# Gathers on GpSimd: rows ahead of values, early messages for 14 row blocks, and a pause behind two of three gathers

## The chip, the cores and the metric

The kernel runs on one core of a Trainium2 chip. The metric is the device time in microseconds of one execution. Work is spread by hand over the engines: PE (TensorE, matrix products), DVE (VectorE), ACT (ScalarE), POOL (GpSimd) and the DMA queues. Each engine works through its own queue of instructions in order and waits on semaphores of the others.

## The reference

Two graph layers over 2708 nodes with 128 features. `adj` is a 2708 x 2708 matrix that is almost empty: a few neighbours a row, each row's non-zero entries equal (one over their number).

```python
# layer 0, for x (2708, 128)
XW = mobius_matvec(W, x)                       # x @ W, rescaled row by row
gamma = 2 / max(1 - sum(XW * XW), eps)
two_mean = (adj @ (gamma * XW)) / clamp(adj @ (gamma - 1))
AXW = mobius_scalar_mul(adj.sum(-1), mobius_scalar_mul(0.5, two_mean))
x = layernorm(x + expmap0(relu(logmap0(AXW))))

# layer 1
s, d = x @ msg_w[:, :D].T, x @ msg_w[:, D:].T
messages = gelu(s[i] + d[j] + msg_b)           # for every pair i, j
aggregated[i] = sum_j messages[i, j] * adj[i, j]
new = concat(x, aggregated) @ upd_w.T + upd_b
x = layernorm(x + layernorm(gelu(new) + x) * ln_w + ln_b)
```

The messages are needed for the non-zero entries of `adj` alone. The kernel finds these entries on the device while it does layer 0, and computes layer 1 edge by edge.

## The kernel before, in words

Rows are cut into 22 blocks of 128.

**Layer 0.** `layer0(b)` loads the transposed block of `adj` (tile `aT`, two buffers, 1.4 MB, on the SyncE queue), multiplies it with `y` in 22 products of 128 x 130 (L369) and writes the block's nominator and denominator into `nom[:, b]` (L374, one VectorE operation a block, which is a handy clock of the progress). ScalarE takes the sign of `aT` (L364).

**Finding the edges.** `keys` turns the signs into numbers that hold column positions (L396 and the following lines) and takes the largest eight of each group (L404). `extract` makes from these a list of edges for the block, in *edge tiles* of 128 edges each: `J` (the neighbour's number), `rid` (the row within the block) and `same` (the weight of the row). Block 0 has 20 such tiles, block 1 has 8, later ones fewer; there are 99. `F` (12 buffers, L501) is the place of each edge in `adj`. A first part of each block's tiles holds only edges to the first ten blocks of columns ("early" tiles, 51 in all); the rest are "late".

**Gathers.** `gather` starts an indirect DMA on GpSimd's queue (L197): each of the 128 partitions fetches from an address of its own. There are two kinds, 99 of each:
- values, `V<-adj,F`: one number for each edge, read back from `adj` and compared at the end with `same`, to make sure that the found edge has the weight that was assumed;
- rows, `dd<-table,J`: 128 numbers for each edge, the neighbour's `d`, out of the DRAM tensor `table`.

Values are gathered at the end of `extract`, as soon as `F` is there. For blocks below `PAUSED` (9) an operation `pow` on a single column (L202, tile `gap`, which nobody reads) is pinned right behind each value gather. Rows are gathered by `fetch`, at most four a call.

**Between the layers.** `layer0_end` runs three times (`CHUNKS`: blocks 0 to 9, 10 to 19, 20 and 21), in parts that are spread between the blocks of layer 0: norms, artanh, tanh and the layer norm, then `s` and `d` for the chunk (L577), then the write of `d` to `table` (L583). After the first chunk the early tiles' rows can be gathered; the late ones need the whole table.

**Layer 1.** `work` is the list of edge tiles in groups of four: first the early tiles of the blocks below `EARLY` (8), then for these the late ones, and for the others all. `messages` takes one group: the row's `s` by a product with the selection matrix `R` (L736), a comparison that makes the weights `rv` (L738), the sum with the gathered rows (L741), Gelu (L742) and the product that sums up each row's edges (L751). For a block below `EARLY` the sum of its early tiles is put by (L755) and goes into the update as an operand of its own. When a block's last tile is done, `node` computes the update (L606 to L610), the layer norms (`first`, `finish`, L600 to L642) and the output. A group's gathered rows stand in one of `RING` = 14 "rooms"; a gather for a later group waits until a room is free.

**The end.** A few sums show whether the edge lists are complete and whether all values are right. If not, a dense branch computes layer 1 anew; with these inputs it isn't taken.

**Order.** The source's order isn't that of the engines. A planner orders the instructions of each engine ahead of time, by their dependencies and by durations that it assumes: an instruction that comes late in the source may stand early in its queue if the planner sees a free place for it. On the chip each queue is then kept in that order. `tc.issue_after` and `tc.high_priority` pin the `pow` behind its gather.

Of the kernel before, what the change touches and what calls it, by code (L numbers as in the profile page):

```python
# [10 lines left out]
F32 = mybir.dt.float32  # L11
U32 = mybir.dt.uint32
BF16 = mybir.dt.bfloat16
F16 = mybir.dt.float16
U8 = mybir.dt.uint8
I32 = mybir.dt.int32
AF = mybir.ActivationFunctionType
OP = mybir.AluOpType
AX = mybir.AxisListType

P = 128
# [7 lines left out]
CHUNKS = [(0, 10), (10, 20), (20, 22)]  # L29
PARTS = (0, 1, 2, 2)  # L30
GROUPS = [(0, 8), (8, 6), (14, 4), (18, 2), (20, 2)]
PAUSED = 9
EARLY = 8
FETCH = 14


# [45 lines left out]
def hyperbolic_then_message_kernel(  # L82
# [10 lines left out]
    nc = tc.nc  # L93
# [6 lines left out]
    LISTS, NT, NC = lists()  # L100
# [6 lines left out]
    sc = ctx.enter_context(tc.tile_pool(name="sc", bufs=1))  # L107
# [5 lines left out]
    w0_sb, wT, rowvec, o = pk[:, :D], pk[:, D : 5 * D].rearrange("p (i d) -> p i d", d=D), {}, 5 * D  # L113
# [6 lines left out]
    for q, (to, of) in enumerate(((xT, x_t), (x_sb.rearrange("p b d -> p (b d)"), x_nm))):  # L120
# [7 lines left out]
    ones_b = const.tile([P, P], BF16, name="ones_b")  # L128
# [3 lines left out]
        tri, ones_b, pattern=[[1, P]], compare_op=OP.is_gt, fill=0.0, base=0, channel_multiplier=-1  # L132
# [37 lines left out]
    V = const.tile([P, NT], F32, name="V")  # L170
    rv_of = const.tile([P, NT, 2], F32, name="rv_of")
    rid, same = rv_of[:, :, 0], rv_of[:, :, 1]
    top = const.tile([P, NC], F32, name="top")
# [18 lines left out]

    gap, half = (const.tile([P, 1], F32, name=f"gap{k}") for k in range(2))
    nc.gpsimd.memset(half, 0.5)

    def gather(o, src, at, pause=False):
        last = nc.gpsimd.indirect_dma_start(  # L197
            out=o, out_offset=None, in_=src, in_offset=bass.IndirectOffsetOnAxis(ap=at, axis=0)
        )
        if pause:  # L200
            with tc.issue_after(last.ins), tc.high_priority():
                nc.gpsimd.tensor_tensor(gap, half, half, op=OP.pow)  # L202

# [6 lines left out]
    def bank(name, bufs=2):  # L210
        return ps.tile([P, 512], F32, name=name, bufs=bufs)

    def flat(t):
        return t.rearrange("p b d -> p (b d)")
# [62 lines left out]
    small = ctx.enter_context(tc.tile_pool(name="small", bufs=2))  # L277
# [35 lines left out]
    for g, n in quads:  # L313
# [5 lines left out]
        t = small.tile([P, 4, D], F32, name="work", bufs=3)  # L319
        nc.vector.tensor_mul(t[:, :n, :], mx[:, g : g + n, :], mx[:, g : g + n, :])  # L320
        nc.vector.tensor_reduce(ss_m[:, g : g + n], t[:, :n, :], axis=AX.X, op=OP.add)
    for b in range(NB):
        t = small.tile([P, D], F32, name="junk")
# [85 lines left out]

    EXP = 0x7F800000  # L410
    known = [-1]

    def extract(l):

        b, groups, c0, wa, wb, t0, n, late = LISTS[l]
        C = wa + wb

        def tmp(name, dt=F32, w=CMAX):
            return small.tile([P, w], dt, name=name, bufs=2 if name in ("m", "whole") else 1)[:, :C]
# [19 lines left out]
        whole = tmp("whole", I32)  # L439
        nc.scalar.copy(whole, tk)  # L440
        op = bank("sel", 1)
        db = small.tile([P, 3], BF16, name="db")
# [7 lines left out]
        for k, _ in parts:  # L450
            first = n - late if k and wa else 0
            dl = deg[:, l, k + 1 : k + 2]
            for k0 in range(first, n, 4):
# [3 lines left out]
                o = flat(R[:, t0 + k0 : t0 + k1, :])  # L457
# [22 lines left out]
        F = small.tile([P, TMAX], U32, name="F", bufs=12)  # L480
        step = 512 // (C + 2)
        for k0 in range(0, n, step):
            k1 = min(n, k0 + step)
            w = k1 - k0
            t = slice(t0 + k0, t0 + k1)
# [15 lines left out]
            nc.vector.scalar_tensor_tensor(  # L501
                F[:, k0:k1], J[:, t], float(b * P * N - 1), rid[:, t], op0=OP.add, op1=OP.add
            )
        for t in range(t0, t0 + n):
            gather(V[:, t : t + 1], adj.rearrange("i (j o) -> (i j) o", o=1), F[:, t - t0 : t - t0 + 1], b < PAUSED)
        known[0] = b

    x1, x1T, gd = x_sb, xT, nom
# [190 lines left out]
    def fours(parts, before):  # L699
        v = [(b, t, t == ts[0], t == ts[-1], before) for b, ts in parts for t in ts]  # L700
        return [v[k : k + 4] for k in range(0, len(v), 4)]

    work = fours([(b, early[b]) for b in range(EARLY)], True)
    ahead = len(work)
    work += fours([(b, late[b] if b < EARLY else early[b] + late[b]) for b in range(NB)], False)
    rooms, sums, whole = [], {}, []
# [3 lines left out]
    order = {v: [(q, k, b, t) for q, ts in enumerate(work) for k, (b, t, *_) in enumerate(ts) if (t in soon) == v]  # L710
             for v in (True, False)}

    def fetch():

        for _ in range(4):
            ready = [v for v in (True, False) if order[v] and order[v][0][0] < done[0] + RING]
            if not whole:
                ready = [v for v in ready if v and order[v][0][2] <= known[0]]
            if not ready:
                return  # L720
            q, k, _, t = order[min(ready, key=lambda v: order[v][0])].pop(0)
            while len(rooms) <= q:
                rooms.append(edge.tile([P, 4, P], F32, name="dd", bufs=RING))
            gather(rooms[q][:, k, :], table[: SPLIT * P] if t in soon else table, J[:, t : t + 1])

    def messages():

        q, ts = done[0], work[done[0]]
        done[0] += 1
        w = len(ts)  # L730
        dd = rooms[q][:, :w, :]
        X = bank("kx" if q >= ahead and q % 2 else "X").rearrange("p (t d) -> p t d", d=D)[:, :w, :]
        rv = edge.tile([P, 4, P], F32, name="rv", bufs=2)
        for k, (b, t, *_) in enumerate(ts):
            for i in range(3):
                nc.tensor.matmul(X[:, k, :], lhsT=R[:, t, :], rhs=s3[:, b, i, :], start=(i == 0), stop=(i == 2))  # L736

            nc.vector.tensor_scalar(  # L738
                rv[:, k, :], iotaN, rid[:, t : t + 1], same[:, t : t + 1], op0=OP.is_equal, op1=OP.mult
            )  # L740
        nc.vector.tensor_tensor(dd, X, dd, op=OP.add)  # L741
        nc.scalar.activation(dd, dd, AF.Gelu)  # L742
        for k, (b, t, first, final, before) in enumerate(ts):
            mine = before or b >= EARLY
            if first:
                while len(sums) > 2:
                    step()
                sums[b] = bank("mp", 3)
                if mine:
                    own(b, sums[b])  # L750
            nc.tensor.matmul(  # L751
                sums[b][:, :P], lhsT=dd[:, k, :], rhs=rv[:, k, :], start=(first and not mine), stop=final
            )
            if final and before:
                nc.scalar.copy(gd[:, b, :D], sums.pop(b)[:, :P])  # L755
            elif final:
                g0, gn = group[b]
                queue.append(node(gd[:, g0 : g0 + gn, :D], b - g0, b, g0, gn, [gd[:, b, :D]] if b < EARLY else []))
        fetch()
        step()  # L760
        step(1)
# [10 lines left out]
    with tc.issue_after(setup.ins):  # L772
        for b in range(NB):
            block = layer0(b)
            next(block)
            go_on(b, 0)
            for x in placed:
                next(x, None)
            placed = []
            next(block)  # L780
            go_on(b, 1)
            for x in found:
                next(x)
            placed, found = found, []
            sgn = next(block)
            for l in of_block[b]:
                keys(l, sgn)
                found.append(extract(l))
            if b == 0 or b == NB - 1:
                for x in found:  # L790
                    next(x)
                    next(x, None)
                for x in placed:
                    next(x, None)
                found, placed = [], []
            if b >= FETCH:
                fetch()
            for b0, b1 in CHUNKS:
                if b == b1 - 1 and b1 < NB:
                    ends.append((b1, layer0_end(b0, b1)))  # L800
                    next(ends[-1][1])
# [7 lines left out]
    for _ in range(RING):  # L809
        fetch()  # L810
# [14 lines left out]
    for _, _, c0, wa, wb, *_ in LISTS:  # L825
# [4 lines left out]
    seconds = [  # L830
        top[:, c0 : c0 + k * (wa + wb)].rearrange("p (k w) -> p k w", w=wa + wb)[:, :, s]
        for c0, _, wa, wb, k in runs
        for s in ([slice(0, 8)] if wa else []) + ([slice(wa + wb - 8, wa + wb)] if wb else [])
    ]
    bad1 = sc.tile([P, len(seconds) + 3], F32, name="bad1")
    for i, v in enumerate(seconds):
        k = v.shape[1]
        f = small.tile([P, NL, 8], F32, name="bits3")[:, :k, :]
# [1 line left out]
        nc.vector.tensor_tensor(f, v, f, op=OP.subtract)  # L840
        nc.vector.tensor_reduce(bad1[:, i : i + 1], f, axis=AX.XY, op=OP.max)
    nc.vector.tensor_reduce(
        bad1[:, -3:-2], top.rearrange("p (k e) -> p k e", e=8)[:, :, 7], axis=AX.X, op=OP.max
    )
    nc.vector.tensor_scalar(bad1[:, :-2], bad1[:, :-2], 256.0, None, op0=OP.is_ge)

    differ = small.tile([P, 4 * P], F32, name="work", bufs=3)[:, :NT]
    nc.vector.tensor_tensor(differ, V, same, op=OP.not_equal)
    nc.vector.scalar_tensor_tensor(differ, rid, 0.0, differ, op0=OP.is_gt, op1=OP.mult)
    nc.vector.tensor_reduce(bad1[:, -2:-1], differ, axis=AX.X, op=OP.max)  # L850
    nc.vector.tensor_reduce(bad1[:, -1:], bad, axis=AX.X, op=OP.max)
    flags = sc.tile([P, 2], F32, name="flags")
    nc.vector.tensor_reduce(flags[:, 0:1], bad1, axis=AX.X, op=OP.max)
# [11 lines left out]
    bp = bank("sel", 1)  # L865
    nc.tensor.matmul(bp[:, 0:2], lhsT=ones, rhs=flags, start=True, stop=True)
    nc.tensor.matmul(bp[:, 2:4], lhsT=ones, rhs=cnt, start=True, stop=True)
    tot = sc.tile([P, 4], F32, name="tot")
# [1 line left out]
    nc.vector.tensor_tensor(tot[:, 2:3], tot[:, 2:3], tot[:, 3:4], op=OP.not_equal)  # L870
    nc.vector.tensor_add(tot[:, 0:1], tot[:, 0:1], tot[:, 1:2])
    nc.vector.tensor_add(tot[:, 0:1], tot[:, 0:1], tot[:, 2:3])
    flag = sc.tile([P, 1], I32, name="flag")
    nc.vector.tensor_copy(flag, tot[:, 0:1])

    while done[0] < len(work):
        messages()
    while queue:
        step()

    dense = nc.values_load(flag[0:1, 0:1], min_val=0, max_val=2 * P + 1)
    with tc.If(dense > 0):
        with tc.tile_pool(name="dn", bufs=1) as dn:
            room = R.rearrange("p t i -> p (t i)").bitcast(F32)
# [99 lines left out]
```

## Time and profile before

| | |
|---|---|
| time | 476.65 us, the median of three (472.91 to 479.4) |
| profiled span | 470.8 us |
| TensorE busy | 293.5 us (62%) |
| VectorE busy | 280.4 us (60%) |
| GpSimd busy | 242.4 us (51%) |
| ScalarE busy | 214.0 us (45%) |
| value gathers (L197) | 99, 998 ns each on GpSimd |
| row gathers (L197) | 99, 958 ns each |
| pauses (L202) | 61, 620 ns each |
| clock that TensorE was granted | 0.787 of full speed |

A gather's duration on GpSimd is the time to make and start its transfers, not the time until the data is there. No engine is busy for much more than six tenths of the span, so what counts is which of them works in which stretch; the prediction goes through this.

### The profile page before, as it was taken

The page shows a single profiled execution, that of the slowest core. Times are in us where ns is not written, and L with a number is a line of the kernel's source. Part 1 is how long each engine was busy: PE and PEld are TensorE (multiplying, and loading weights), DVE is VectorE, ACT ScalarE, POOL GpSimd, SP SyncE. Part 2 cuts the span into 40 slices and gives each one's busy share as a digit, 9 for nine tenths or more (in the row PEclk, how much of TensorE's full clock was granted, in tenths as well). Part 3 has the DMA queues.
Part 4 walks back from the last instruction along what each step waited for, and adds up shares of the span by engine and source line. Part 5 has one row for each costly group of instructions (what it writes and reads, how often), then busy time and mean ns, then how long its engine had stood idle before and what let it go on. Part 6 is the DMA issues. An engine that isn't in the chain of part 4 may idle for free.

```text
span 470.8 us, 8239 instructions
## 1 busy us (share of the span) xinstructions
PE 293.5 (62%) x2603; PEld 261.0 (55%) x2603; DVE 280.4 (60%) x1580; ACT 214.0 (45%) x609; POOL 242.4 (51%) x353
## 2 busy tenths in 40 slices
PE   4249999999999931252738947655300713999840
PEld 4139988999979820142627946544200712897730
DVE  0997998868979602022224779974000411799995
ACT  2953868786959802031324773932000201334441
POOL 6200888988888877735754400226776475200000
PEclk9758999999999965568957996859555665899865
DMA  8403544646644431122413300101211121100111
GB/s 335 207 1 124 194 179 135 236 142 230 222 172 158 161 117 37 28 79 95 151 28 141 126 1 24 34 11 45 52 50 50 30 54 36 24 1 4 43 37 43
DMA packets 16029, 45.15 MB, mean 96 GB/s; under 512 B 5418, under 2 KB 10942, under 8 KB 13166
## 3 DMA queue, kind: packets, MB, share of 16 engines
q1 hardware_dynamic: 9502, 37.43, 21.8%
q0 software_dynamic: 6336, 6.55, 5.6%
q10 hardware_dynamic: 144, 0.60, 0.4%
q8 instruction: 22, 0.36, 0.3%
q14 instruction: 25, 0.20, 0.1%
HBM read 41.74 MB, written 2.83 MB: 95 GB/s over the span
## 4 chain that ended last, share of the span: by engine, by line
PE 35%; DVE 27%; another core or an unknown queue 24%; ACT 6%; issue 5%; DMA 1%; DVEq 0%; ACTq 0%
PE mp L369 17%; PE kx L396 4%; PE mp L751 3%; DVE rv L738 2%; PE X L577 2%; DVE top L404 2%; PE sel L489 2%; DVE st L600 1%; PE X L736 1%; DMA xT<-in_x_t_dram 1%; DVE dd L741 1%; DVE nom L624 1%; PE kx L317 1%; PE sel L608 1%
## 5 line engine op out<-in xcount | busy, mean ns | idle before, releaser
L197 POOL DMA_INDIRECT V<-in_adj_dram,F x99 | 98.8, 998 | 108.5 <-DVE F L501 70.1
L369 PE MATMUL mp<-y,aT 128*128 128x130 f32 x968 | 141.7, 297 | 15.1 <-issue 14.8
L369 PEld LDWEIGHTS mp<-y,aT 128*128 128x128 f32 x968 | 127.1, 205 | 16.5 <-issue 16.3
L197 POOL DMA_INDIRECT dd<-table_dram,J x99 | 94.8, 958 | 47.8 <-issue 45.7
L364 ACT ACTIVATE sgn<-aT 128x2816 bf16<-128x2816 f32 x22 | 56.0, 2547 | 2.3 <-DMA aT<-in_adj_t_dram 2.1
L738 DVE TENSOR_SCALAR rv<-iotaN,rv_of 128x128 f32<-128x128 f32 x99 | 30.1, 347 | 42.8 <-PE X L736 34.2
L404 DVE MAX8 top<-kx 128x8 f32<-128x128 f32 (+3 forms) x133 | 25.3, 227 | 30.0 <-remote 25.4
L751 PE MATMUL mp<-rv,dd 128*128 128x128 f32 x198 | 35.7, 334 | 11.2 <-ACT dd L742 11.2
L489 PE MATMUL sel<-z,R 128*128 128x42 bf16 (+5 forms) x297 | 19.5, 194 | 31.6 <-issue 17.3
L202 POOL TENSOR_TENSOR gap<-gap 128x1 f32<-128x1 f32 x61 | 37.8, 620 | 1.5
L751 PEld LDWEIGHTS mp<-rv,dd 128*128 128x128 f32 x198 | 30.8, 236 | 13.4 <-ACT dd L742 12.1
L396 PE MATMUL kx<-kd,sgn 128*128 128x128 bf16 x484 | 32.9, 223 | 8.1 <-ACT sgn L364 8.1
L396 PEld LDWEIGHTS <-sgn 128*128 128x128 bf16 x484 | 28.1, 99 | 14.6 <-ACT sgn L364 8.5
L489 PEld LDWEIGHTS <-R 128*128 128x128 bf16 x297 | 15.2, 98 | 35.6 <-issue 19.6
L689 PE MATMUL mp<-ident,nom 128*128 128x128 f32 x44 | 10.0, 322 | 39.2 <-ACT nom L755 39.2
L494 DVE TENSOR_TENSOR work<-sel,place 128x120 f32<-128x120 f32 (+11 forms) x29 | 11.1, 382 | 37.4 <-remote 32.4
L742 ACT ACTIVATE dd<-dd 128x512 f32<-128x512 f32 (+2 forms) x26 | 15.8, 607 | 30.6 <-DVE dd L741 17.9
L456 ACT ACTIVATE away<-iota,mid 128x256 f16<-128x256 f32 (+3 forms) x54 | 28.7, 572 | 1.7 <-DVE mid L449 0.6
L689 PEld LDWEIGHTS mp<-ident,nom 128*128 128x128 f32 x44 | 7.1, 208 | 40.1 <-ACT nom L755 39.6
L736 PEld LDWEIGHTS <-R 128*128 128x128 bf16 x297 | 21.4, 108 | 12.4 <-issue 10.6
L755 ACT COPY nom<-mp 128x128 f32<-128x128 f32 x8 | 2.1, 262 | 46.8 <-remote 43.4
L408 ACT ACTIVATE junk_s<-kx 128x384 bf16<-128x384 f32 (+2 forms) x25 | 12.2, 486 | 18.2 <-DVE top L404 14.1
(224 smaller groups left out, 599.3 us busy)
## 6 DMA issues: line engine op xcount, KB each, us to landing
aT<-in_adj_t_dram SPq DMA_DIRECT2D x22, 1408.0 KB
V<-in_adj_dram,F POOLq DMA_INDIRECT x99
dd<-table_dram,J POOLq DMA_INDIRECT x99
xT<-in_x_t_dram SPq DMA_DIRECT2D x2, 704.0 KB
x_sb<-in_x_nm_dram SPq DMA_DIRECT2D x2, 704.0 KB
table_dram<-dt SPq DMA_DIRECT2D x4, 256.0 KB
out_dram<-nom SPq DMA_DIRECT2D x4, 256.0 KB
pk<-in_pack_dram ACTq DMA_DIRECT2D x1, 587.5 KB
```

What stands on the lines that cost most here:

```text
L197: last = nc.gpsimd.indirect_dma_start(out=o, out_offset=None, in_=src, in_offset=bass.IndirectOffsetOnAxis(ap=at, axis=0))
L202: nc.gpsimd.tensor_tensor(gap, half, half, op=OP.pow)
L364: nc.scalar.activation(sgn, aT, AF.Sign, accum_out=signs[:, b : b + 1])
L369: p = nc.tensor.matmul(op[:, : D + 2], lhsT=aT[:, j, :], rhs=y[:, j, :], start=(j == 0), stop=(j == NB - 1))
L396: nc.tensor.matmul(kp[:, i * P : (i + 1) * P], lhsT=sgn[:, j, :], rhs=kd[:, q, :], start=False, stop=(i == len(groups) - 1 and j == j1 - 1),)
L404: nc.vector.max(top[:, c : c + 8], seg[:, s, :])
L456: nc.scalar.activation(r0, iota[:, k0 * P : k1 * P], AF.Abs, scale=2.0, bias=mid[:, k : k + 1])
L489: nc.tensor.matmul(sp[:, k, :], lhsT=R[:, t0 + k0 + k, :], rhs=z[:, i, :], start=(i == 0), stop=(i == 2))
L689: nc.tensor.matmul(ag[:, :P], lhsT=gd[:, b, :D], rhs=ident, start=True, stop=False)
L736: nc.tensor.matmul(X[:, k, :], lhsT=R[:, t, :], rhs=s3[:, b, i, :], start=(i == 0), stop=(i == 2))
L738: nc.vector.tensor_scalar(rv[:, k, :], iotaN, rid[:, t : t + 1], same[:, t : t + 1], op0=OP.is_equal, op1=OP.mult)
L751: nc.tensor.matmul(sums[b][:, :P], lhsT=dd[:, k, :], rhs=rv[:, k, :], start=(first and not mine), stop=final)
```

## The change

Four things are changed together.

1. **Pauses.** The `pow` no longer goes by the block: every gather counts, values and rows, and two of three get a `pow` behind them.
2. **Early messages** for the first 14 blocks instead of 8 (`EARLY`), and six row gathers for each block from block 14 on instead of four.
3. **Values last.** Only blocks below `AT_ONCE` (12) gather their values in `extract`. The others wait in a list, `values`: one is taken in each block from block 14 on, one in each free turn of `fetch` when no row is left, and the rest after the last group of messages.
4. **The check of the values**, which stood among the other checks, moves behind all messages and nodes, and reaches the flag by a small product of its own.

```diff
-PAUSED = 9
-EARLY = 8
+AT_ONCE = 12
+EARLY = 14
...
-    def gather(o, src, at, pause=False):
+    gathers = [0]
+    def gather(o, src, at):
...
-        if pause:
+        gathers[0] += 1
+        if gathers[0] % 3:
             with tc.issue_after(last.ins), tc.high_priority():
                 nc.gpsimd.tensor_tensor(gap, half, half, op=OP.pow)
...
+    values = []
+    def value(n):
+        for _ in range(min(n, len(values))):
+            t, at = values.pop(0)
+            gather(V[:, t : t + 1], adj.rearrange("i (j o) -> (i j) o", o=1), at)
...
-        for t in range(t0, t0 + n):
-            gather(V[:, t : t + 1], ..., F[:, t - t0 : t - t0 + 1], b < PAUSED)
+        values.extend((t, F[:, t - t0 : t - t0 + 1]) for t in range(t0, t0 + n))
+        if b < AT_ONCE:
+            value(n)
...
-    def fetch():
-        for _ in range(4):
+    def fetch(n=4):
+        for _ in range(n):
...
             if not ready:
-                return
+                if whole and not any(order.values()):
+                    value(1)
+                continue
...
             if b >= FETCH:
-                fetch()
+                fetch(6)
+                value(1)
...
-    differ = ...                     # V against same, among the other checks
-    nc.vector.tensor_reduce(bad1[:, -2:-1], differ, axis=AX.X, op=OP.max)
...
-    nc.vector.tensor_copy(flag, tot[:, 0:1])
     while done[0] < len(work):
         messages()
+    value(NT)
     while queue:
         step()
+    differ = ...                     # the same two operations
+    nc.vector.tensor_reduce(other[:, 0:1], differ, axis=AX.X, op=OP.max)
+    bp = bank("sel", 1)
+    nc.tensor.matmul(bp[:, 0:1], lhsT=ones_b, rhs=other[:, 0:1], start=True, stop=True)
+    nc.vector.tensor_tensor(flag, bp[:, 0:1], tot[:, 0:1], op=OP.add)
```

More of the change, by code (lines that the diff above doesn't have):

```diff
@@ L503, in extract @@
             )
-        for t in range(t0, t0 + n):
-            gather(V[:, t : t + 1], adj.rearrange("i (j o) -> (i j) o", o=1), F[:, t - t0 : t - t0 + 1], b < PAUSED)
+        values.extend((t, F[:, t - t0 : t - t0 + 1]) for t in range(t0, t0 + n))
+        if b < AT_ONCE:
+            value(n)
         known[0] = b
@@ L834, in hyperbolic_then_message_kernel @@
     ]
-    bad1 = sc.tile([P, len(seconds) + 3], F32, name="bad1")
+    bad1 = sc.tile([P, len(seconds) + 2], F32, name="bad1")
     for i, v in enumerate(seconds):
@@ L842, in hyperbolic_then_message_kernel @@
     nc.vector.tensor_reduce(
-        bad1[:, -3:-2], top.rearrange("p (k e) -> p k e", e=8)[:, :, 7], axis=AX.X, op=OP.max
+        bad1[:, -2:-1], top.rearrange("p (k e) -> p k e", e=8)[:, :, 7], axis=AX.X, op=OP.max
     )
[L845 to L849, printed above, removed]
-    nc.vector.tensor_reduce(bad1[:, -2:-1], differ, axis=AX.X, op=OP.max)
+    nc.vector.tensor_scalar(bad1[:, :-1], bad1[:, :-1], 256.0, None, op0=OP.is_ge)
     nc.vector.tensor_reduce(bad1[:, -1:], bad, axis=AX.X, op=OP.max)
@@ L872, in hyperbolic_then_message_kernel @@
     nc.vector.tensor_add(tot[:, 0:1], tot[:, 0:1], tot[:, 2:3])
-    flag = sc.tile([P, 1], I32, name="flag")
-    nc.vector.tensor_copy(flag, tot[:, 0:1])
     while done[0] < len(work):
         messages()
+    value(NT)
     while queue:
         step()
-    dense = nc.values_load(flag[0:1, 0:1], min_val=0, max_val=2 * P + 1)
+    differ = small.tile([P, 4 * P], F32, name="work", bufs=3)[:, :NT]
+    nc.vector.tensor_tensor(differ, V, same, op=OP.not_equal)
+    nc.vector.scalar_tensor_tensor(differ, rid, 0.0, differ, op0=OP.is_gt, op1=OP.mult)
+    other = small.tile([P, 3], BF16, name="db")
+    nc.vector.tensor_reduce(other[:, 0:1], differ, axis=AX.X, op=OP.max)
+    bp = bank("sel", 1)
+    nc.tensor.matmul(bp[:, 0:1], lhsT=ones_b, rhs=other[:, 0:1], start=True, stop=True)
+    flag = sc.tile([P, 1], I32, name="flag")
+    nc.vector.tensor_tensor(flag, bp[:, 0:1], tot[:, 0:1], op=OP.add)
+    dense = nc.values_load(flag[0:1, 0:1], min_val=0, max_val=3 * P + 1)
     with tc.If(dense > 0):
```

## The prediction

> **What bounds the kernel now.** I read the slices of the page first, then the busy time by stretch, then the GpSimd timeline, then the DMA queues.
>
> ```profile
> PE   4249999999999931252738947655300713999840
> DVE  0997998868979602022224779974000411799995
> POOL 6200888988888877735754400226776475200000
> ```
>
> Forty slices of 11.8 us. TensorE and VectorE are full up to slice 13 (about 160 us), then both fall to a few tenths, recover, fall to zero in slices 28 to 30 and recover. GpSimd stands at seven to nine tenths up to slice 15, and in the later dips it is the only one of the three at work. The table by stretch puts numbers on it:
>
> ```profile
> 100.00:160.00 60.00, 59.11 (x603) 54.82 (x602) 50.15 (x305) 48.82 (x132) 53.44 (x66) 1.00 0.55 194
> 162.00:277.00 115.00, 56.60 (x471) 50.12 (x469) 35.65 (x229) 35.28 (x97) 66.36 (x69) 0.72 0.25 86
> 319.00:367.00 48.00, 8.88 (x78) 8.10 (x75) 6.58 (x21) 2.77 (x8) 33.28 (x35) 0.60 0.18 48
> 404.00:471.00 67.00, 45.45 (x387) 39.13 (x385) 59.80 (x339) 25.28 (x74) 0.19 (x1) 0.83 0.08 24
> ```
>
> The columns are TensorE, its weight loads, VectorE, ScalarE, GpSimd (busy us and instructions), then clock, DMA share and GB/s. Before 160 everything runs; from 319 to 367 nothing but GpSimd does; from 404, when the last gather has been issued, VectorE is full again. What changes at 160 is visible on GpSimd:
>
> ```profile
> 157.66 0.99 POOL L197 DMA_INDIRECT V<-in_adj_dram,F  x1 [0.17 <-issue]
> 158.68 0.59 POOL L202 TENSOR_TENSOR gap<-gap 128x1 f32<-128x1 f32 x1
> 159.44 0.99 POOL L197 DMA_INDIRECT V<-in_adj_dram,F  x1 [0.17 <-DVE z L474]
> 160.74 0.96 POOL L197 DMA_INDIRECT V<-in_adj_dram,F  x1 [0.30 <-issue]
> 162.00 0.95 POOL L197 DMA_INDIRECT V<-in_adj_dram,F  x1 [0.30 <-issue]
> ```
>
> Until 159.44 each gather has a power operation behind it; then they follow one another. The waits say that nobody waits for data in the bad stretches: "issue" and "remote" are waits that the profile can't put down to any work. The DMA view of 319 to 367 (first fence) and of 60 to 110 (second) shows what is missing:
>
> ```profile
> DMA packets 1120, 2.30 MB, mean 47 GB/s; under 512 B 560, under 2 KB 560, under 8 KB 1120
> q0 software_dynamic: 1120, 2.30, 17.7%
> ```
>
> ```profile
> q0 software_dynamic: 954, 0.02, 1.4%
> q8 instruction: 5, 0.08, 0.7%
> q14 instruction: 3, 0.02, 0.1%
> ```
>
> With paced gathers eight instruction packets land in 50 us; in 49 us of unpaced ones, none. So engines run out of instructions while gathers go back to back. Runs of three (259.00 to 261.51, 267.67 to 270.18) stall nothing: TensorE is 10.00 of 10 us busy from 260 to 270. Runs of six and more do: 248.04 to 254.40, and VectorE waits 4.3 us until 255.09.
>
> **What the Trainium skill says.** "Runtime: NRT & Kernel Launch", Instruction fetch mechanics: engines stream their instructions through a DMA queue in blocks of 16 KiB, a cost that it calls mostly hidden. The trace has 22 packets with 0.36 MB on q8, which is 16 KB each, but from 160 to 404 the cost isn't hidden. "DMA: Bandwidth & Descriptors", Queues, rings and completion order: each DMA engine takes turns between queue rows, packet by packet. That alone would not starve a row: the gathers took 17.7% of the engines' time. So the trace shows that it happens and not why, and I don't lean on a mechanism.
>
> **The loss now.** The nominator of block 15 (L374) is written at 162.28 and that of block 21 at 277.30. By the same line blocks 2 to 12 took 5.5 to 9.2 us each, and blocks 14 and 15 took 7.1 and 8.6; at 7.9 us the six blocks end at 162.3 + 47.4 = 209.7: 67.6 us lost. From 320 to 400 VectorE, which bounds that work, is busy 15 us of 80: 65 lost. Together 133 us over the 137 gathers without a pause, 0.97 us each.
>
> **The change, part by part.**
>
> Pacing. All 198 gathers count, so 132 get a power operation and 66 do not. From the timeline: with a pause 61 gathers took 47.61 to 159.44, 1.83 us each (about 1.79 where VectorE is quiet); without, 35 took 318.89 to 361.69, 1.26 each. A cycle of three costs 2 x 1.83 + 1.26 = 4.92 in the busy stretch, 1.62 a gather in the quiet one; I take 1.63. So GpSimd needs 198 x 1.63 = 323 us where it needed 61 x 1.83 + 137 x 1.26 = 284. If no gap opens, it runs from the first F at 47.6 to **370**. This becomes the floor. Streams of values and rows are interleaved, each with its own pattern, so runs without a pause should stay at two or three, the length that stalled nothing.
>
> Does a gap open? The 62nd value gather, block 9's, finds its F at 147.58 and comes up at 47.6 + 61 x 1.63 = 147: no gap. Early rows follow (the first part of the table is written from about 139 on). Before the end of layer 0, 44 tiles of rows are fetched where there were 32 (six a block from block 14; of the 51 early tiles 7 lie in groups beyond the 14 rooms). With 71 values at once and 8 to 28 late ones that is work for GpSimd until 47.6 + 123 x 1.63 = 248, or 281 with all values.
>
> Layer 0. With instructions flowing, block 21 ends at 210. In the kernel before, from there to the first row of the whole table it took 277.3 to 318.9, 41.6 us, nearly all of it busy VectorE work (36.89 of 42 us from 277 to 319). The same work ends at 251. So GpSimd is not kept waiting, and 30 us of slack remain if the values stand ahead.
>
> Early messages for 14 blocks. The groups go from 26 to 25, one addition, Gelu and fetch less (0.69 + 0.63 us), and six more copies of a sum (L755, 0.26 us each) and six more update products (two L608 passes, 0.6 us together at the most): hidden, since the tail waits for gathers: four take 6.5 us, and VectorE's message work of four tiles (4 x 0.34 + 0.69 us) plus its nodes some 3 to 4 (59.8 us for the last 13 Gelu groups and all finishing).
>
> Late values. 28 of 99 are issued as filler. The order on GpSimd is the planner's, not the source's: before, rows written late in the source ran ahead of the values of blocks 10 to 16. By the same habit ready values will be put ahead of rows that wait for the table, so I expect late rows, not values, at the end. The value check moves to the end: two VectorE operations of 0.25 us, a reduction of 0.24, one 128x1 product (0.16, from L445) and an addition in place of a copy: under 2 us after the last value lands, and on the path only if values are last.
>
> The end. The last gather is issued at 370. For landing I take 2 us, the fixed time of a transfer in "DMA: Bandwidth & Descriptors", Anatomy of one DMA; no row here shows it for a gather. Before, the last dd addition began at 448.31 and the kernel ended at 470.8, 22.5 us with three groups finishing at once; with fewer I take 20. Sum: 370 + 2 + 20 = 392 us span. The median of the times lies 5.9 us over the profiled span (476.65 against 470.8), so **398 us**.
>
> **Rivals.**
> - *Values last.* If the 20 values left after layer 0 really come behind all rows, messages end at about 370 - 20 x 1.63 + 22 = 359 and the check closes at 370 + 2 + 4 = 376, so 382 us. For it: that is the order of the source. Against: the planner's filling.
> - *Two in a row still starve somewhat.* If each of the 66 unpaced gathers still costs 0.97 us: 48 of them before 281, 46 us, so the table comes at 297, GpSimd waits 16 us, ends at 386, and the last messages lose some 5: 386 + 22 + 5 + 6 = 419. For it: no stretch shows pairs between pauses. Against: runs of three did no harm.
> - *Pauses of one help nothing unless they follow every gather.* All 198 gathers then cost 0.97 us where 137 did: 61 x 0.97 = 59 us longer, about 536: slower. Against it: stretches of three gathers.
> - *GpSimd's longer queue only takes the place of the stalls*, with rooms for rows (14 groups) blocking it: some 470. Against: compute needs 3 to 4 us per group of 6.5.
>
> **How the numbers follow.** Main case 0.48 (398), values last 0.22 (382), partial starvation 0.19 (419), no net gain 0.04 (470), slower 0.07 (536). A range from 379 (values last, GpSimd at 1.62) to 430 (partial, with a pair costing a quarter more) leaves out the last two and edges, about 0.15 to 0.2. Faster by over 2%: 0.89; within 2%: 0.04; slower: 0.07.
>
> **What would show it.** Right: L202 132 times; GpSimd busy almost without a break from 48 to about 370 with about 1.63 us a gather; block 21's L374 near 210; instruction packets through the whole run; TensorE above seven tenths up to slice 17 or so; the last rows, not values, at the end. Wrong: TensorE slices near zero while pairs are issued, L374 of block 21 beyond 240, or GpSimd idle for tens of us for F, J or rooms, which would mean that another wait bounds the end.

## The result, and the profile after

The changed kernel takes 402.65 us (median of four, 399.82 to 404.57), the kernel before beside it 476.53. The ratio is 0.845, with an interval of 0.837 to 0.853. The profiled span is 398.1 us. The forecast was 398, in a range of 379 to 430.

One thing has to be known before the experiments are read. The kernel before takes 474 to 479 us in some sessions on the chip, the one above among them, and 363 to 364 in others; within a session its times lie within 3% of each other in the first kind and, one of 411.2 us apart, within about 1% in the second. The same chip gave 363.06 in one session and 473.98 in another. I call them *starving* and *quiet* sessions. The names are labels: what the engines lack in a starving session isn't shown. Each ratio below is against the kernel before in the same session.

The slices of the page, 9.95 us each, answer to those of before:

```profile
PE   3418989999989999736999646441045999996800
DVE  0898989977669978615778899940014788998992
POOL 6400288888888875778888888877888888888800
```

GpSimd (POOL) is now busy almost without a break until its gathers end. Where VectorE had long holes, two are left: around slice 17 and in slices 27 to 29, counted from 0. The table by stretch (TensorE, weight loads, VectorE, ScalarE, GpSimd; then clock, DMA share, GB/s) shows what lies around them:

```profile
160.00:180.00 20.00, 10.92 (x112) 9.86 (x112) 6.67 (x39) 8.00 (x21) 16.14 (x19) 0.92 0.47 167
180.00:226.00 46.00, 41.90 (x431) 39.09 (x432) 33.98 (x219) 33.94 (x90) 40.20 (x50) 0.92 0.46 158
280.00:292.00 12.00, 1.00 (x10) 1.00 (x10) 1.02 (x2) 1.02 (x3) 10.35 (x13) 0.50 0.15 38
330.00:369.00 39.00, 35.24 (x308) 30.15 (x308) 34.42 (x171) 17.13 (x52) 33.31 (x41) 0.99 0.21 50
369.00:398.00 29.00, 7.72 (x36) 5.75 (x34) 21.46 (x160) 7.41 (x21) 8.21 (x14) 0.56 0.15 41
```

Rows two and four are the change at work: while gathers go in the pattern pause, pause, none, TensorE is busy 41.90 us of 46, and 35.24 of 39 at the end, where in the kernel before it had 8.88 of 48. Rows one and three lie in the two holes. The GpSimd timeline shows what runs in the first (the dots stand for lines left out):

```profile
165.84 1.01 POOL L198 DMA_INDIRECT dd<-table_dram,J  x1 [0.18 <-issue]
167.15 0.96 POOL L198 DMA_INDIRECT dd<-table_dram,J  x1 [0.30 <-issue]
...
175.96 0.95 POOL L198 DMA_INDIRECT V<-in_adj_dram,F  x1 [0.30 <-issue]
176.94 0.58 POOL L204 TENSOR_TENSOR gap<-gap 128x1 f32<-128x1 f32 x1
```

This is a run of nine gathers without a pause between them, seven of rows and two of values. VectorE and ScalarE stand for 6.16 and 9.96 us there, and TensorE, which needs a result of VectorE, for 8.61 us, until 181.99. In the second hole 21 value gathers and one of rows run unpaced from 253.51 to 281. VectorE's timeline has this there:

```profile
268.30 0.43 DVE L597 TENSOR_TENSOR nom<-sf,dt 128x256 f32<-128x256 f32 x1
290.25 0.69 DVE L753 TENSOR_TENSOR dd<-X,dd 128x512 f32<-128x512 f32 x1 [21.52 <-remote]
290.86 0.41 DVE L286 TENSOR_TENSOR work<-sf,s 128x256 f32<-128x256 f32 x1
300.18 0.69 DVE L753 TENSOR_TENSOR dd<-X,dd 128x512 f32<-128x512 f32 x1 [8.90 <-remote]
```

"remote" is again a wait that the profile can put down to no work: 30.4 us of VectorE in two pieces. The rows that these two additions (L753) need aren't what is missing: in a quiet session the same two ran without a wait, at 246.51 and 247.50. So what stopped the engines before is still there where the pauses are missing. It also outlasts the unpaced run: GpSimd paces its gathers again from 281.01 on, while VectorE stands until 290.25, and once more until 300.18. The pauses are missing because a planner orders the queue: it moved gathers ahead to fill a place that it saw as free, and their `pow` operations stayed behind. Fourteen of the 132 stand behind the very last gather.

### The profile page after: what moved, and what is told of

The parts are those of the page before. It is cut to its first block, busy times and chain, and to the rows that moved or that the text cites. A ratio compares the mean times of both kernels' runs of the same rounds, so it can differ in the third digit from the quotient of the medians.

```text
span 398.1 us, 8353 instructions
## 1 busy us (share of the span) xinstructions
PE 281.0 (71%) x2616; PEld 250.3 (63%) x2616; DVE 281.4 (71%) x1579; ACT 215.7 (54%) x614; POOL 288.5 (72%) x424
## 5 line engine op out<-in xcount | busy, mean ns | idle before, releaser
L371 PE MATMUL mp<-y,aT 128*128 128x130 f32 x968 | 132.0, 287 | 1.2 <-DMA aT<-in_adj_t_dram 0.7
L371 PEld LDWEIGHTS mp<-y,aT 128*128 128x128 f32 x968 | 119.4, 196 | 1.8 <-DMA aT<-in_adj_t_dram 0.8
L198 POOL DMA_INDIRECT dd<-table_dram,J x99 | 98.3, 993 | 22.4 <-issue 19.8
L204 POOL TENSOR_TENSOR gap<-gap 128x1 f32<-128x1 f32 x132 | 81.3, 616 | 4.3
L748 PE MATMUL X<-s,R 128*128 128x128 bf16 x213 | 19.8, 239 | 25.7 <-DVE dd L753 21.1
L763 PE MATMUL mp<-rv,dd 128*128 128x128 f32 x198 | 32.9, 315 | 6.5 <-ACT dd L754 4.5
L750 DVE TENSOR_SCALAR rv<-iotaN,rv_of 128x128 f32<-128x128 f32 x99 | 30.7, 352 | 9.2 <-PE X L748 4.5
L754 ACT ACTIVATE dd<-dd 128x512 f32<-128x512 f32 (+1 forms) x25 | 15.6, 624 | 34.6 <-DVE dd L753 22.0
L763 PEld LDWEIGHTS mp<-rv,dd 128*128 128x128 f32 x198 | 28.2, 217 | 8.8 <-ACT dd L754 5.9
L753 DVE TENSOR_TENSOR dd<-X,dd 128x512 f32<-128x512 f32 (+1 forms) x18 | 12.2, 675 | 30.4 <-remote 30.4
L498 PEld LDWEIGHTS <-R 128*128 128x128 bf16 x297 | 15.3, 97 | 21.8 <-DVE m L445 8.8
L579 PE MATMUL kx<-ident,x_sb 128*128 128x128 f32 x22 | 5.6, 360 | 13.8 <-DVE x_sb L576 13.8
```

The lines of the kernel that those rows point to most:

```text
L198: last = nc.gpsimd.indirect_dma_start(out=o, out_offset=None, in_=src, in_offset=bass.IndirectOffsetOnAxis(ap=at, axis=0))
L371: p = nc.tensor.matmul(op[:, : D + 2], lhsT=aT[:, j, :], rhs=y[:, j, :], start=(j == 0), stop=(j == NB - 1))
L498: nc.tensor.matmul(sp[:, k, :], lhsT=R[:, t0 + k0 + k, :], rhs=z[:, i, :], start=(i == 0), stop=(i == 2))
L750: nc.vector.tensor_scalar(rv[:, k, :], iotaN, rid[:, t : t + 1], same[:, t : t + 1], op0=OP.is_equal, op1=OP.mult)
L763: nc.tensor.matmul(sums[b][:, :P], lhsT=dd[:, k, :], rhs=rv[:, k, :], start=(first and not mine), stop=final)
```

## The experiments

The theory on record: gathers that follow one another without a pause keep the other engines from getting instructions; the pauses end that; and GpSimd's own queue is the floor that takes its place. Rivals: the new order of rows and values carries the gain; or any instruction between two gathers would do.

| kernel | quiet session | starving session |
|---|---|---|
| before | 363.55, 362.77, 363.06 | 476.53, 479.0, 478.74, 473.98, 478.38 |
| changed | 398.51 (1.099) | 402.65 (0.845) |
| pauses alone (before, with the new pauses) | 402.39, 402.4 (1.110, 1.108) | 421.6 (0.893) |
| order alone (changed, with the old pauses) | 367.28, 367.74 (1.011, 1.014) | 481.42 (1.007) |
| changed, memset behind each gather | 358.78 (0.987) | 521.09 (1.095) |
| changed, no pause at all | 356.31 (0.981) | not run |
| changed, a `pow` behind each gather | not run | 426.93 (0.891) |
| changed, order pinned | 391.66 (1.082) | not run |

**Pauses alone.** The kernel before, with the pauses counted as in the change:

```diff
-        if pause:
+        gathers[0] += 1
+        if gathers[0] % 3:
```

> The kernel before, with the pauses of the changed one (every gather counts, two of three get a power operation) and nothing else of the change. Theory (pauses let the other engines get instructions; the order of the gathers matters little): most of the gain, 400 to 420 us, block 21's nominator near 230, some 30 us of it in short stalls where the planner leaves seven to nine gathers without a pause. Rival (the gain comes from rows first and more early messages): 460 us or more.

> The kernel before with the pauses counted as in the change (behind two of three gathers), its order of gathers kept: the first experiment again. Theory A (on a chip where the kernel before takes about 477 us, unpaced gathers keep instructions from the other engines, and the pauses alone are what the change gains): 395 to 415 us there, ratio about 0.85; where the kernel before takes about 364, 402 again. Rival B (the new order carries half of the gain): 435 or more on a chip with 477.

> The kernel before with the pauses counted as in the change, its order of gathers kept, once more, for a chip on which the kernel before takes about 477 us. Theory A (there the pauses are the whole gain): 395 to 415 us, ratio about 0.84. Rival B (pauses only help together with the order): 435 or more. Where the kernel before takes about 364 us, 402 as twice before, and nothing is told apart.

The first two fell in quiet sessions: 402.39 and 402.4 us, ratios 1.110 (1.104 to 1.115) and 1.108 (1.103 to 1.112). The first time lies in its forecast of 400 to 420 us by luck, since nothing was there to repair. In a quiet session the pauses do nothing but lengthen GpSimd's queue; gathers go on until 375.5 in the second. The third fell in a starving session: 421.6 us, 0.893 (0.887 to 0.899), between the forecasts of its two theories. So the pauses alone give 52 us there, of the changed kernel's 74. What they lack shows in GpSimd's timeline of that run:

```profile
263.48 2.06 POOL L205 TENSOR_TENSOR gap<-gap 128x1 f32<-128x1 f32 x3
278.83 1.01 POOL L199 DMA_INDIRECT V<-in_adj_dram,F  x1 [13.29 <-DVE F L504]
```

With the old order the planner formed four unpaced runs, of 9, 8, 7 and 5 gathers. TensorE waited 8.00 and 12.05 us, until 182.25 and 199.44, at the ends of the first two and beyond them, the table's last part came at 294.5 instead of 267.8, and GpSimd ran dry for 13.29 us, waiting for the `F` of a late block. In the changed kernel GpSimd's longest gap is 4.4 us; it has more early rows and held-back values to put there.

**Order alone.** The changed kernel with the old pauses, behind the first 61 value gathers:

```diff
-        gathers[0] += 1
-        if gathers[0] % 3:
+        if pause:                    # t < 61, for values alone
```

> The changed kernel with the pauses of the kernel before (behind the 61 value gathers of blocks 0 to 8 alone). Theory: 137 gathers follow one another without a pause as before, so 455 to 485 us with TensorE and VectorE idle during the runs. Rival (order): 400 to 430 us.

> The changed kernel with the pauses of the kernel before, behind the first 61 value gathers alone: the second experiment again. Theory A: where the kernel before takes about 477 us, 137 gathers still go without a pause and cost the others about 0.97 us each, so 460 to 490, ratio about 1; where it takes about 364, 367 again. Rival B (rows first, values last fill the gaps and carry part of the gain): 410 to 450 on a chip with 477.

> The changed kernel with the pauses of the kernel before, behind the first 61 value gathers alone, once more, for a chip on which the kernel before takes about 477 us. Theory A (there the pauses are the gain and the order is none): 460 to 490 us, ratio about 1, TensorE near zero through the run of rows at the end. Rival B (the order carries part of the gain): 410 to 450. Where the kernel before takes about 364 us, 367 as twice before, and nothing is told apart.

In quiet sessions 367.28 and 367.74 us, which tells nothing apart; in a starving one 481.42: 1.007 (1.004 to 1.011) of the kernel before. The order alone gains nothing; together with the pauses it is worth 421.6 to 402.65, put as ratios 0.893 to 0.845. So the two parts are not a sum: the order is worth something only on top of the pauses.

The last two runs are the same kernel in both kinds of session, so the difference can be looked at by itself. In each, 29 row gathers, one every 1.26 us, fill 36 us. First the stretch in the quiet session, then in the starving one (columns as above):

```profile
292.00:328.00 36.00, 32.98 (x293) 28.00 (x292) 28.11 (x134) 12.59 (x39) 27.46 (x29) 1.00 0.22 52
```

```profile
333.00:369.00 36.00, 5.07 (x35) 4.49 (x34) 2.81 (x8) 0.80 (x2) 27.47 (x29) 0.62 0.22 52
```

GpSimd does the same work in the same time, and the DMA share (0.22) and the rate (52 GB/s) agree to the digit. TensorE has 32.98 us of work in the one and 5.07 in the other. The engines aren't slower, they stand: an addition of rows takes 0.68 to 0.69 us in both. The DMA view differs in the instruction packets; the quiet stretch:

```profile
q0 software_dynamic: 896, 1.84, 21.9%
q8 instruction: 2, 0.03, 0.5%
q14 instruction: 1, 0.01, 0.1%
```

and the starving one, where no queue but the gathers' moved a packet:

```profile
q0 software_dynamic: 908, 1.89, 22.5%
```

From such views I read, in the kernel before, that instructions don't arrive while gathers follow one another. But an engine that stands asks for none either, and the times of the packets speak against it. Both traces hold the same 22 and 26 instruction packets (q8 and q14). In the starving one no packet starts between 328 and 378 us, and yet engines come back to work in between:

```profile
337.00 0.69 DVE L752 TENSOR_TENSOR dd<-X,dd 128x512 f32<-128x512 f32 x1 [3.86 <-remote]
344.14 0.27 ACT L766 COPY nom<-mp 128x128 f32<-128x128 f32 x1 [11.44 <-remote]
359.57 0.69 DVE L752 TENSOR_TENSOR dd<-X,dd 128x512 f32<-128x512 f32 x1 [8.69 <-issue]
374.31 0.27 ACT L766 COPY nom<-mp 128x128 f32<-128x128 f32 x1 [29.37 <-remote]
```

As far as the packets show, what they ran had been fetched by 328, so a late packet isn't what ended these waits. At 374.31 all engines come back, 6 us after the last gather that GpSimd started (368.36) before it had to wait for a room. The kernel before looks alike: no packet from 318 to 374, ScalarE back at 366.75, and GpSimd's last gather ahead of that at 361.69. So it is shown that unpaced gathers stop the engines in these sessions, and not by what.

The starving session costs 481.42 - 367.5 = 114 us; spread over 137 unpaced gathers that is 0.83 us each. For the kernel before it is 476.5 - 363.1 = 113 over 137, 0.83 again.

**A short operation as the pause.**

```diff
-        if gathers[0] % 3:
+        if gathers[0]:
...
-                nc.gpsimd.tensor_tensor(gap, half, half, op=OP.pow)
+                nc.gpsimd.memset(gap, 0.5)
```

> The changed kernel with a memset of one column behind every gather in place of a power operation behind two of three. GpSimd's memset of a column took 0.09 us in the kernel before. Theory A (the pause works by its length): a tenth of a microsecond does little, TensorE stalls as before, 440 to 490 us. Theory B (any instruction between two gathers breaks the run): no stalls, GpSimd at about 1.35 us a gather and done near 315, so 345 to 365 us.

> The changed kernel with a memset of one element a partition (about 0.09 us) behind every gather in place of the power operation behind two of three: the third experiment again. Theory A (what lets the engines fetch is idle time between the gathers' issues, so a short operation gives too little): in a session where the kernel before takes about 477 us, 450 to 540 us, with stalls of the other engines whenever gathers run. Rival B (any other instruction between two gathers is enough, however short): 355 to 375 there, faster than both kernels. Where the kernel before takes about 364 us, 359 as before, and nothing is told apart.

In the quiet session 358.78 us, 0.987 (0.984 to 0.991). In the starving one 521.09, 1.095 (1.084 to 1.105): rival B falls, and this is slower than the kernel before. GpSimd's timeline there says why:

```profile
153.17 0.95 POOL L198 DMA_INDIRECT V<-in_adj_dram,F  x1 [5.90 <-DVE F L510]
154.11 0.11 POOL L204 MEMSET gap<- 128x1 f32 x1
154.42 0.95 POOL L198 DMA_INDIRECT V<-in_adj_dram,F  x1 [0.19 <-issue]
```

The memset fits into the 0.3 us that lie between two gathers anyway: the pitch is 154.42 - 153.17 = 1.25 us, as with nothing there. Behind a `pow` it is about 1.78. So it is no pause, and now the first 61 gathers stop the engines too: from 50 to 160 us TensorE is busy 81.8 us, against 106.5 in the quiet session. The cost, 521.1 - 358.8 = 162 us over 198 gathers, is 0.82 us each, the third time the same number.

**A `pow` behind every gather.**

```diff
-        if gathers[0] % 3:
+        if gathers[0]:
```

> The changed kernel with a power operation behind every gather, 198 in place of 132. Theory A (GpSimd's own queue is the floor): 66 more operations at 0.56 to 0.61 us each lengthen the queue by 37 to 40 us where it never waits, so gathers end at about 405 and the kernel takes 428 to 440 us, on any chip. Rival B (pauses pay by letting the other engines fetch instructions, and fewer unpaced runs pay more): under 400 us. Rival C (the floor is the other engines' work, and the queue is hidden): about 400, no change.

A starving session: 426.93 us, 0.891 (0.885 to 0.897), in place of 0.845. More pauses, and slower: the floor is GpSimd's queue.

```profile
393.32 0.99 POOL L198 DMA_INDIRECT dd<-table_dram,J  x1 [0.17 <-issue]
394.35 0.58 POOL L204 TENSOR_TENSOR gap<-gap 128x1 f32<-128x1 f32 x1
395.10 0.99 POOL L198 DMA_INDIRECT dd<-table_dram,J  x1 [0.17 <-issue]
```

The last gather starts at 395.10, 27.1 us later than in the changed kernel, and the kernel takes 24.3 us longer, though the table's last write came 9 us earlier (258.7). I had expected gathers to about 405 and 428 to 440 us: I missed that the planner leaves two runs unpaced here too (8 and 13), and the pitch in the row stretch is 1.78, not the 1.83 of the busy one.

**No pause at all.**

```diff
-        if gathers[0] % 3:
+        if gathers[0] > 1000:
```

> The changed kernel itself, in the same company as the other runs. Theory A (with its power operations GpSimd's own queue is the floor, 46.9 + 198 x 1.63 = 370, and the end chain takes some 29): about 400 us on any chip, with gathers to about 370. If the kernel before takes about 364 us here, the ratio is 1.10; if it takes about 476, 0.84. Rival B (the two planned runs of 9 and of 22 gathers without a pause stall the other engines everywhere, and hold the end up by some 10): 400 too, but then VectorE waits over 15 us for nothing that the profile names during the run of 22; by A on a chip where the kernel before takes 364, nothing waits there.

> The changed kernel without any power operation. Theory A (a pause only pays where unpaced gathers starve the engines): where the kernel before takes about 364 us, gathers cost 1.26 us each, so GpSimd's queue alone would end at 47 + 198 x 1.26 = 296; the rows of the whole table, 48 or more behind a table at about 251, end at 312 or later, and with 29 us of end chain the kernel takes 325 to 350 us, under both kernels. Where the kernel before takes about 476 us, all 198 gathers cost the others 0.97 us each: 500 to 540. Rival B (pauses are needed on every chip for instruction fetch): above 400 us on both.

Both ran in one quiet session. The changed kernel takes 398.51 us, 1.099 (1.095 to 1.103). Without its pauses it takes 356.31, 0.981 (0.978 to 0.985), the lowest time of all, if above the 325 to 350 forecast; its last gather starts at 323.0, some way above the 296 of the queue alone, because GpSimd waits 21.8 us for `F`, until 147.52, and the late rows wait for the table. So in a quiet session 42 us of the changed kernel are pauses that nobody needs.

The changed kernel's trace in the quiet session also shows a wait that the standing engines cover in the other. Of VectorE's timeline:

```profile
248.31 0.43 DVE L288 TENSOR_TENSOR s<-work,s 128x256 bf16<-128x256 f32 x1
278.12 0.26 DVE L890 TENSOR_TENSOR work<-V,rv_of 128x99 f32<-128x99 f32 x1 [29.38 <-DMA V<-in_adj_dram,F]
278.30 1.11 DVE L750 TENSOR_SCALAR rv<-iotaN,rv_of 128x128 f32<-128x128 f32 x4
```

L890 is the comparison of all values. In the source it stands behind all messages; in VectorE's queue the planner put it ahead of the additions of 21 of the 25 groups, so VectorE stands 29.38 us until the last of the 21 hoisted values has landed, and the rows come behind these values anyway. Theory A, by which nothing waits there, was wrong in that, and rival B half right: VectorE does wait more than 15 us at the run of 22 in a quiet session, but for values, which the profile names.

**The order pinned.** Each gather is held behind the gather or the `pow` before it, so that the queue is as the source has it:

```diff
+        with ExitStack() as pinned:
+            if behind:
+                pinned.enter_context(tc.issue_after(behind[0]))
...
+        behind[:] = [last.ins]
...
-                nc.gpsimd.tensor_tensor(gap, half, half, op=OP.pow)
+                behind[:] = [nc.gpsimd.tensor_tensor(gap, half, half, op=OP.pow).ins]
```

> The changed kernel with every gather pinned behind the one before it or its pause, so that GpSimd runs them in the order of the source: never more than two without a pause, values last. Theory (the two stalls left, 173 to 181 and 270 to 290, come from the runs of 9 and 22 gathers that the planner moved ahead without their pauses): both stalls vanish, block 21's nominator near 212, GpSimd ends at 368 to 372 with values, and the kernel at 380 to 390 us. Rival (the stalls are waits for data, or GpSimd alone sets the end): 398 to 405 us, no change.

A quiet session: 391.66 us, 1.082 (1.075 to 1.088), against 1.099 for the unpinned one. The two stalls that the forecast of 380 to 390 us was to end aren't there in a quiet session, so it isn't tested by this. No run is longer than two, and twenty values now really come last. The last gather starts at 371.69, 6.8 us later than in the unpinned kernel, yet the end follows after 16.5 us instead of 30.7. VectorE's timeline shows what these 16.5 us are:

```profile
374.46 0.26 DVE L894 TENSOR_TENSOR work<-V,rv_of 128x99 f32<-128x99 f32 x1 [18.01 <-DMA V<-in_adj_dram,F]
374.64 0.30 DVE L244 TENSOR_SCALAR rh<-ve 128x2 int32<-128x2 int32 x3
```

The comparison stands in the queue ahead of the finishing of the last nodes (L244 and on), 18.01 us idle, and then they run one after another. Had it stood behind them, part of them could have been done by then; that wasn't tried. In a starving session this kernel wasn't tried, so what the two unpaced runs cost there is only bounded: the changed kernel takes 402.65 in a starving session and 398.51 in a quiet one, some 4 us for all that is left of the difference.

No version was seen to beat both kernels in both kinds of session. In the starving ones the changed kernel is the fastest that was run, in the quiet ones the one without pauses.

## Why the prediction was right, and where it was not

**Pacing, the floor: right.** The forecast was 198 gathers at 1.63 us, from 47.6 to 370. Measured: 46.92 to 367.97, (367.97 - 46.92) / 197 = 1.63. The page's row is the predicted count:

```profile
L204 POOL TENSOR_TENSOR gap<-gap 128x1 f32<-128x1 f32 x132 | 81.3, 616 | 4.3
```

That this is the floor, and not just a coincidence, the run with a pause behind each gather shows: 27.1 us more of queue, 24.3 us more of time.

**"So engines run out of instructions": not shown.** The packets were counted rightly, eight in 50 us and none in 49. But they come where the program has got to, and the waits end without one, as the two stretches above show. The forecast didn't need this step: it needed that unpaced gathers stop the engines and paced ones don't.

**"Runs without a pause should stay at two or three": wrong.** They do in the source. The queue has runs of 9 and 22, because a hoisted gather leaves its `pow` behind. The prediction argued from the planner's filling in one step (late values) and forgot it in this one. Cost: block 21's nominator (L376) comes at 226.3 instead of 210, of which 12 us fall on block 16 (19.9 us long, in the quiet session 7.8), and the table's last write at 267.8, where 251 was forecast for the first row gathered behind it. In the quiet session they come at 206.7 and 245.6, so without the stalls the step would have held.

**The 41.6 us from block 21 to the table: right within 3 us.** To the issue of the table's last write it took 41.5, where it took 39.0 in the kernel before and 38.9 in the quiet session; the 41.6 ran to the first row gathered behind it, 2.6 us later. The 30 us of slack that the prediction gave GpSimd took up the delay of some 19 us: the gathers end only 3.1 us later than in the quiet session (364.86).

**Values: half right.** Rows are last, as forecast; the last value gather starts at 278.77. But the check of the values was priced as under 2 us after the last value, "on the path only if values are last". It stands in the middle of VectorE's queue and holds up what is behind it: 29.38 us in the quiet session; in the other it comes behind the 30.4 us in which VectorE stands anyway, and VectorE comes to it at 301.2 with all values landed. Beside the floor it cost little, since the gathers behind those values set the end.

**The end: 8 us too small.** Landing and end chain were put at 2 + 20. From the last gather's start to the last addition of rows (372.97) it took 5.0 us, and from there to the end 25.1. The 2 us came from the Trainium skill, "DMA: Bandwidth & Descriptors", Anatomy of one DMA, for lack of a row; the trace has one now: an addition that waited for its rows ran at 366.81, for a gather that started at 363.04, 3.8 us before. VectorE is busy 21.46 us of the last 29, finishing nodes. The holes aren't the reason: in the quiet session, where VectorE waits for rows again and again before that, it is busy 20.92 us of the last 29 and the end follows 25.7 us after the last addition. So this work is left for the end there too. In exchange the times lie 4.6 us over the span and not 5.9. Sum: 368.0 + 5.0 + 25.1 + 4.6 = 402.7.

**The loss per unpaced gather: 0.97 forecast, 0.82 to 0.83 measured.** The other 20 of the 133 us that I counted on before's trace aren't lost to the gathers: a quiet session doesn't give them back.

**Rivals.** Pairs between pauses don't stop the engines: from 330 to 369 TensorE is busy 35.24 us of 39. Values last (382) didn't happen, and where it was forced, the end was 16.5 us behind the last gather and not 6, for the check's place in the queue. The slower rival (every gather costs the others, 536) came not with this change but with the memset: 521.

**What the pauses are worth in general** the prediction didn't see: its 79 us of gain are the repair of a loss that some sessions have and some don't. In a quiet session the same change costs 10%. The changed kernel's own time follows from the floor in both kinds (402.65 and 398.51); that it is a gain was luck of the session, as far as the prediction knew.

The skill's "Runtime: NRT & Kernel Launch", Instruction fetch mechanics, calls the cost of the fetch mostly hidden. The runs agree for quiet sessions, where TensorE is busy 32.98 us of 36 beside unpaced gathers. Whether the fetch has a part in the 5.07 us of the starving session no run here shows.

## What to carry to other kernels

Where several engines fall silent at once and the trace names no work that they wait for, look at what is issued meanwhile, and test it with the same kernel in several sessions before a repair is paid for: here the repair gains 15% or costs 10%. A count that falls while the engines stand (here that of instruction packets) can be what follows, so compare its times with those at which they start again. The `pow` changed the pitch of the gathers and helped; the memset fitted into a gap that was there and did nothing. And where a planner orders the queues, a pair of instructions is only kept together if both directions are pinned, and a check that is written last may still be queued in the middle, so read the order off the trace.

## What the runs showed of the hardware

- While gathers of 128 elements or rows are issued every 1.25 to 1.26 us, the other engines stand for most of the time in some sessions (TensorE busy 5.07 us of 36) and not in others (32.98 of 36), at the same DMA share and rate; one and the same chip had sessions of both kinds. Spread over these gathers, the loss is 0.82 to 0.83 us each. A pitch of 1.26, 1.78 and 1.78 in turn ends it (TensorE busy 35.24 us of 39), after a long unpaced run up to 19 us later. What stops the engines, what makes a session of the one kind or the other, and whether it is the time between two issues that helps or something else in the `pow`, stays open: no operation of another kind and the same length was tried.
- A gather of rows had landed 3.8 us after its start on GpSimd, of which 0.94 was GpSimd's own time; a gather of values 2.5 us after its start (275.64 to 278.12 in the quiet session).
